# Layer 2 of a four-layer network: two fp32r parts of the projection weights instead of three bf16 parts, and one fp32r pass for dt

## The chip, the cores and the metric

The kernel runs on one core of a Trainium2 chip. The time is that of the device, in microseconds (us), from the first to the last instruction; less is better. Engines are TensorE (PE, matmuls; PEld is its weight load), VectorE (DVE), ScalarE (ACT), GpSimd (POOL) and SyncE (SP, which here only issues DMAs). ACT issues the DMAs of the set-up as well.

## The reference

Four layers follow one another on an input of 4 batches, 128 channels and 64 x 64 pixels. Layer 0 is attention over the 4096 pixels, layer 1 two quantized 3 x 3 convolutions, layer 2 a selective scan over the pixels as a sequence ("mamba"), layer 3 attention again. The change lies in layer 2:

```
xz = x @ W_in                                  # 128 -> 2 * 256
xh, z = split(xz, 2)
xh = silu(xp[:-1] * w[:, 0] + xp[1:] * w[:, 1] + b)   # causal convolution, two taps; xp is xh, padded
x_dbl = xh @ W_x                               # 256 -> 8 + 16 + 16
dt_low, Bmat, Cmat = x_dbl[:8], x_dbl[8:24], x_dbl[24:40]
dt = softplus(dt_low @ W_dt + b_dt)            # 8 -> 256
A = -exp(A_log)
h = exp(dt * A) * h + dt * Bmat * xh           # step by step, 16 states for each of 256 channels
y = (sum over the states of h * Cmat + xh * D) * silu(z)
x = silu(group_norm(y @ W_out)) + x_hsi
```

The input x of layer 2 is what layer 1 left: integers from 0 to 15 (divided by 15), which the kernel keeps exactly in fp8.

## The kernel before

Set-up (lines 161 to 335): constants are loaded on the DMA queue of ACT, in the order of the program, and prepared on DVE. `load_layer2` (L296) multiplies the first half of W_in by each of the two taps of the convolution, so that the projection and the convolution are one product over two shifted inputs, and splits the result `wf` (two tap products and the z half, 768 columns) into three bf16 parts `w3` (L309 to L312). `wf` and `cwb` take the two buffers of the tag "ud" in the pool `mam`. `w_dt` is cleared by POOL and gets W_dt twice, once for each half of a token block (L325 to L328).

The main part has no loops on the device. Generators describe chains of operations: `energies`, `exponentials`, `products`, `accumulations`, `parts` and `finish` for both attention layers; `convolutions` for layer 1; `preparation`, `decays`, `scans`, `lasts`, `additions` and `output` for layer 2; `images`, `fetches` and `stage_input` for DMAs. Each operation is announced by `op(engine, time, *needs)` with a time in us that the programmer put down. The class `Order` (L48) keeps a clock for each engine. Again and again it takes the operation with the earliest possible start, plus 0.15 times the rank of its chain, and emits it (L80 to L112). So the order on every engine is written at build time from these entries, and each engine then executes its list strictly in that order. The entry is no more than a planner's figure; if it changes, the order of everything changes. `bank=True` marks users of the one PSUM bank `ps_g`, of which only one is in work at a time; `port=True` keeps an operation of DVE off the operations of POOL.

Attention runs in stages of 64 blocks: (0, 0), (0, 1), (0, 2), (3, 0), (0, 3), (3, 1), (3, 2), (3, 3), given as (layer, batch). A block is eight energy products (L492), two exponentials on ACT (L511, 128 x 1024 each), eight products with v (L560) and, unless DVE adds the terms up (L533, only in the first eight column blocks and in the last stage), sums by matmul (L580). Four blocks make a column block of 256 queries, two column blocks an eviction (L606, L608) with sums turned into reciprocals: L627 on PE, L636 on DVE (`rall`), L640 on PE, L648 on DVE, and for layer 3 the output product L659 and L663. Stage (3, 3) needs x2 of batch 3, the output of layer 2 for the last batch.

Layer 2 goes through 32 token blocks of 512 (8 for each batch), each with 16 scan steps, one for each state. A scan step on DVE is the product with B (L1007), the product with C of the step before (L997) and two scans of 512 (L1015), with two decays on ACT ahead of them (L980) and an addition on POOL behind (L1032). `preparation` (L773) makes what a token block needs:

- z of the token block before: three bf16 products for each half of the channels (L764), copied by ACT (L787);
- xh of this one: six bf16 products for each half, with bias by ACT (L806), then Silu for both (L811, L814);
- x_dbl: eight instructions (L821); ACT copies it to `xd` (L830), SP writes B and C to DRAM (L835), from where `fetches` spreads them over the partitions (L967);
- dt: for each channel half two products of 256 tokens with `w_dt` (L851), in fp32, where one product appears as two instructions in the trace; softplus by ACT (L859 to L868) and DVE (L870 to L878).

`output` multiplies by W_out (`yo`, L894); after eight token blocks of a batch comes the group norm with Silu (L943), and x2 is written to DRAM (L958), from where `stage_input` reads it as `x_in` (L376).

## Time and profile before

| | us |
|---|---|
| median of 3 runs (3644.84 to 3651.89) | 3644.98 |
| span of the profiled execution | 3652.0 |
| PE busy, share of the span | 3375.5, 92% |
| DVE busy | 3124.9, 86% |
| ACT busy | 2505.9, 69% |
| POOL busy | 1317.5, 36% |
| scans of layer 2 on DVE (L1015), both forms | 1250.4 |
| energies and products of attention on PE (L492, L560, L580) | 2730.9 |
| products of the input projection (L764) | 148.3 |
| products for dt (L851) | 70.6 |

The profile shows one execution, whose span is the time meant in the prediction's sum. A group's line gives the line of the kernel, the engine, the operation, what it writes and reads, the shapes (for a matmul rows*columns of the weights first, then output columns and type), the count, then busy time in us and the mean of one in ns; behind the second bar stands how long the engine was idle just before such instructions, and what ended that. Matmuls overlap, so that count times mean is more than their busy time. A line of a timeline gives start and duration in us, engine, line, operation and count, in brackets the idle time ahead of it. A line of the waits gives total, times and longest. PEclk is the granted clock of PE as a share of full speed.

### The profile page before, as it was taken

To read this page: it belongs to the slowest core of one execution; us is meant where nothing else is said; L and a number is where in the kernel's file an instruction comes from. 1 tells how busy PE (TensorE), PEld (TensorE's weight loads), DVE (VectorE), ACT (ScalarE), POOL (GpSimd) and SP (SyncE) were. 2 spreads that over 40 slices of the span, in tenths; PEclk is the share of its full clock that TensorE was granted. 3 is DMA by queue.
4 is the path that set the end of the run, shared out by engine and by line. 5 is a ranking of instruction groups with operands and counts; after the bars stand their busy time and mean duration, and the time that the engine had idled before them with its cause. 6 is when DMAs were issued, how large, how long until landed. Compare 5 with 4: busy or idle time off the path is not lost.

```text
span 3652.0 us, 70191 instructions
## 1 busy us (share of the span) xinstructions
PE 3375.5 (92%) x29559; PEld 2217.0 (61%) x29559; DVE 3124.9 (86%) x2944; ACT 2505.9 (69%) x3655; POOL 1317.5 (36%) x567
## 2 busy tenths in 40 slices
PE   5999989999999899999988999999989999999998
PEld 3776656666666666655555666665555555565665
DVE  3369999999999999999999999999989999982333
ACT  3467777777677777777776777767777777864443
POOL 0014334444434444444444444443434444440000
PEclk8999999999999999999999999999999999999999
DMA  2013344343434434544433333333445544331000
GB/s 71 1 48 94 91 109 98 88 97 93 105 91 117 92 91 98 116 106 108 109 111 120 95 92 90 87 98 91 108 115 114 128 104 111 103 95 58 13 19 17
DMA packets 203655, 327.78 MB, mean 90 GB/s; under 512 B 50609, under 2 KB 53441, under 8 KB 203329
## 3 DMA queue, kind: packets, MB, share of 16 engines
q1 hardware_dynamic: 196384, 322.09, 35.4%
q8 instruction: 234, 3.83, 0.4%
q10 hardware_dynamic: 6944, 1.10, 0.2%
q14 instruction: 93, 0.75, 0.1%
HBM read 304.27 MB, written 18.87 MB: 88 GB/s over the span
## 4 chain that ended last, share of the span: by engine, by line
PE 50%; DVE 32%; ACT 9%; issue 6%; DMA 2%; ACTq 0%; DVEq 0%; SPq 0%
PE us L560 21%; DVE hs L1015 13%; PE e L492 12%; DVE hs L1007 7%; PE us L580 6%; DVE hs L997 5%; ACT da L980 2%; ACT p L511 2%; PE proj L463 2%; PE conv L675 1%; PE xh L764 1%; PE proj L421 1%; PE sc L627 1%; PE yo L894 1%; PE sc L640 1%
## 5 line engine op out<-in xcount | busy, mean ns | idle before, releaser
L1032 POOL TENSOR_TENSOR y<-y,hs 128x1024 f32<-128x1024 f32 x512 | 1219.6, 2382 | 1960.6 <-DVE hs L997 1941.9
L560 PE MATMUL us<-p,v 128*32 128x256 f32 (+1 forms) x12288 | 1519.1, 389 | 103.0 <-ACT p L511 74.1
L560 PEld LDWEIGHTS us<-p,v 128*32 128x32 f32 (+1 forms) x12288 | 1001.7, 138 | 519.2 <-issue 134.5
L511 ACT ACTIVATE p<-e 128x1024 f32<-128x1024 f32 x1024 | 1003.6, 1018 | 330.1 <-PE e L492 259.9
L1015 DVE TENSOR_TENSOR_SCAN hs<-da,hlast,hs 128x512 f32<-128x512 f32 x896 | 1100.8, 1264 | 15.7 <-ACT da L980 15.5
L980 ACT ACTIVATE da<-dt,amat 128x512 f32<-128x512 f32 x1024 | 703.1, 691 | 349.7 <-DVE hs L1015 346.0
L997 DVE TENSOR_TENSOR hs<-hs,bc 128x1024 f32<-128x1024 f32 x512 | 663.4, 1296 | 15.7 <-ACT hlast L990 15.5
L1007 DVE TENSOR_TENSOR hs<-ud,bc 128x1024 f32<-128x1024 f32 x512 | 661.4, 1292 | 0.2
L492 PE MATMUL e<-it,v 64*128 64x256 f32 x4096 | 529.2, 398 | 12.0 <-ACT p L511 11.1
L492 PEld LDWEIGHTS e<-it,v 64*128 64x128 f32 x4096 | 382.2, 191 | 160.8 <-issue 93.9
L580 PE MATMUL us<-p,ones 128*32 128x256 f32 x7040 | 471.0, 385 | 0.0
L580 PEld LDWEIGHTS us<-p,ones 128*32 128x32 f32 x7040 | 201.3, 110 | 189.0 <-issue 73.6
L492 PE MATMUL e<-it,j 64*128 64x256 f32 x2048 | 196.8, 309 | 12.0 <-ACT p L511 10.3
L492 PEld LDWEIGHTS e<-it,j 64*128 64x128 f32 x2048 | 140.9, 189 | 107.9 <-issue 71.6
L533 DVE TENSOR_TENSOR acc<-p 128x1024 f32<-128x1024 f32 x24 | 29.4, 1225 | 200.7 <-PE us L580 176.0
L533 DVE TENSOR_TENSOR acc<-p,acc 128x1024 f32<-128x1024 f32 x96 | 117.6, 1225 | 73.2 <-ACT p L511 68.2
L990 ACT COPY hlast<-hs 128x2 f32<-128x2 f32 x448 | 85.6, 191 | 122.7 <-DVE hs L1015 120.0
L1015 DVE TENSOR_TENSOR_SCAN hs<-da,hs 128x512 f32<-128x512 f32 x128 | 149.6, 1204 | 2.8 <-ACT da L980 2.7
L764 PEld LDWEIGHTS <-w 128*128 128x128 bf16 x576 | 52.5, 99 | 104.2 <-issue 61.9
L764 PE MATMUL xh<-x,w 128*128 128x512 fp8e4 x384 | 94.9, 383 | 7.9 <-ACT sz L787 4.2
L463 PE MATMUL proj<-L_conv_wvT,x_in 128*128 128x128 f32 (+1 forms) x512 | 71.3, 298 | 27.5 <-DVE it L408 17.8
L1036 POOL TENSOR_TENSOR y<-y,sz 128x1024 f32<-128x1024 f32 x32 | 94.4, 2951 | 2.5
(158 smaller groups left out, 2577.2 us busy)
## 6 DMA issues: line engine op xcount, KB each, us to landing
bc<-bc_d SPq DMA_DIRECT2D x512, 512.0 KB, 5.0
x_in<-in_x SPq DMA_DIRECT2D x16, 512.0 KB, 5.1
xpad<-in_x SPq DMA_DIRECT2D x32, 256.0 KB, 3.3
x_d<-yo SPq DMA_DIRECT2D x32, 256.0 KB, 3.0
x_in<-x_d SPq DMA_DIRECT2D x16, 512.0 KB, 6.3
o<-x_d SPq DMA_DIRECT2D x32, 256.0 KB, 5.2
out<-o SPq DMA_DIRECT2D x32, 256.0 KB, 2.0
bc_d<-xd SPq DMA_DIRECT2D x64, 32.0 KB, 1.8
```

The source lines that it names most:

```text
L463: nc.tensor.matmul(to[:, k * d : (k + 1) * d], lhsT=x[:, k // 4, k % 4 * P : (k % 4 + 1) * P], rhs=wv, start=True, stop=True,)
L492: nc.tensor.matmul(e[k % 4 // 2][:, k % 2, k // 4, :], lhsT=jts[s][row : row + D3, col : col + P], rhs=its[s][row : row + D3, c * CB : (c ...
L511: nc.scalar.activation(p, es[t][h], AF.Exp)
L533: nc.vector.tensor_add(accs[k], ps[t, h], other)
L560: nc.tensor.matmul(us[rows, 0, :], lhsT=vts[s][:, 8 * q + k, cols], rhs=ps[t, h][:, k % 2, k // 4, :], start=q == 0 and k < (1 if layer == ...
L580: nc.tensor.matmul(us[32 * m : 32 * m + 32, 1, :], lhsT=ones[:, 0:32], rhs=term, start=False, stop=q == NQ - 1 and k >= len(terms) - 4,)
L764: nc.tensor.matmul(g, lhsT=w3[:, k // len(rhs), lhs[k % len(rhs)] : lhs[k % len(rhs)] + P], rhs=x[:, rhs[k % len(rhs)]], start=(k == 0), s ...
L980: nc.scalar.activation(da, live["in", g][0][:, h, :], AF.Exp, scale=amat[:, h, n : n + 1])
L997: nc.vector.tensor_mul(hs, hs, bcs.pop(m)[:, 1:2, :].to_broadcast([P, 2, TB]))
L1007: nc.vector.tensor_mul(hs, ud, bcs[m][:, 0:1, :].to_broadcast([P, 2, TB]))
L1015: nc.vector.tensor_tensor_scan(hs[:, h, :], das.pop((m, h)), hs[:, h, :], hlast[:, n, h : h + 1] if g % NTB else 0.0, ALU.mult, ALU.add,)
L1032: nc.gpsimd.tensor_tensor(y, y, hss.pop(m), ALU.add)
```

## The change

The weights `wf` are split into two parts in fp32r, the high one rounded to this format and the low one the rest. The input goes to fp32r as well: ACT copies the 512 tokens of z and the 513 of xh from fp8 into `xf`, which takes the buffer "sp". z then needs two products for each half, xh four.

For dt, W_x has the eight columns of dt_low four times, so that x_dbl holds four equal groups of eight rows for each half of the block. ACT writes `xh` (the fp32r-rounded value in the groups where `lowx` is 1, zero elsewhere), DVE subtracts it from `xd` into `xp` in fp32r: high parts in two groups, low parts in the two others. `w_dt` has the high part of W_dt for two groups and the low part for the two others, so that one fp32r product adds all four combinations. The set-up gets the loads and operations that make this `w_dt`; its temporaries `wd` and `wh` take the buffers "ud" of `wf` and `cwb`. The clearing of `w_x` goes, since all its columns are now loaded. The running sum of attention, `acc`, shares the buffer "h". The planner's entries for z, xh and dt on PE become 0.5, 0.95 and 0.3 us.

```diff
--- before.py
+++ after.py
@@ -7,8 +7,6 @@
 from concourse._compat import with_exitstack
 
 F32 = mybir.dt.float32
-BF16 = mybir.dt.bfloat16
-
 FP8 = mybir.dt.float8e4
 
 
@@ -31,6 +29,7 @@
 DI = 256
 DS = 16
 DTR = 8
+RBC = 4 * DTR
 EPS = 1e-5
 LEVELS = 15.0
 
@@ -248,9 +247,8 @@
         nc.vector.tensor_mul(r, r, t)
 
     bn, wint = [], []
-    w3 = const.tile([P, 3, 3 * DI], BF16, tag="w3", name="w3")
+    w2 = const.tile([P, 2, 3 * DI], F32R, tag="w2", name="w2")
     w_x = const.tile([P, 2, D3], F32, tag="w_x", name="w_x")
-    nc.gpsimd.memset(w_x, 0.0)
     w_out = const.tile([P, 2, P], F32, tag="w_out", name="w_out")
     amat = const.tile([P, 2, DS], F32, tag="amat", name="amat")
 
@@ -306,14 +304,12 @@
         nc.vector.tensor_mul(wf[:, 0, :], wf[:, 1, :], cwb[:, 0, :])
         nc.vector.tensor_mul(wf[:, 1, :], wf[:, 1, :], cwb[:, 1, :])
         f = wf.rearrange("p a b -> p (a b)")
-        for k in range(3):
-            nc.vector.tensor_copy(w3[:, k, :], f)
-            if k < 2:
-                nc.vector.tensor_sub(f, f, w3[:, k, :])
-        nc.scalar.dma_start(
-            out=w_x[:, :, 0 : DTR + 2 * DS],
-            in_=i["L2_conv_W_x"].rearrange("(h p) r -> p h r", p=P),
-        )
+        nc.vector.tensor_copy(w2[:, 0, :], f)
+        nc.vector.tensor_sub(w2[:, 1, :], f, w2[:, 0, :])
+        wx = i["L2_conv_W_x"].rearrange("(h p) r -> p h r", p=P)
+        for k in range(4):
+            nc.scalar.dma_start(out=w_x[:, :, DTR * k : DTR * (k + 1)], in_=wx[:, :, 0:DTR])
+        nc.scalar.dma_start(out=w_x[:, :, RBC:D3], in_=wx[:, :, DTR : DTR + 2 * DS])
         nc.scalar.dma_start(out=w_out, in_=i["L2_conv_W_out"].rearrange("(h p) c -> p h c", p=P))
         nc.scalar.dma_start(out=amat, in_=i["L2_conv_A_log"].rearrange("(h p) n -> p h n", p=P))
         nc.scalar.activation(amat, amat, AF.Exp)
@@ -322,10 +318,27 @@
     load_layer1()
     load_layer2()
 
-    w_dt = const.tile([P, 2, DI], F32, tag="w_dt", name="w_dt")
-    nc.gpsimd.memset(w_dt, 0.0)
+    lowx = const.tile([P, 1], F32, tag="lowx", name="lowx")
+    nc.vector.tensor_reduce(
+        lowx, ident.rearrange("p (a k b) -> p k a b", k=2, b=DTR)[:, 1], AX.XY, ALU.add
+    )
+    w_dt = const.tile([P, 2, DI], F32R, tag="w_dt", name="w_dt")
+    wd = mam.tile([P, 2, DI], F32, tag="ud", name="wd", bufs=2)
+    wh = mam.tile([P, 2, DI], F32R, tag="ud", name="wh", bufs=2)
+    mhi, mlo = (const.tile([P, 1], F32, tag=k, name=k) for k in ("mhi", "mlo"))
+    nc.vector.tensor_reduce(
+        mlo, ident.rearrange("p (a k b) -> p k a b", k=2, b=2 * DTR)[:, 1], AX.XY, ALU.add
+    )
+    nc.vector.tensor_scalar(mhi, mlo, -1.0, 1.0, ALU.mult, ALU.add)
+    nc.gpsimd.memset(wd, 0.0)
     for k in range(2):
-        nc.scalar.dma_start(out=w_dt[k * D3 : k * D3 + DTR, k, :], in_=i["L2_conv_W_dt"])
+        for j in range(4):
+            r = k * D3 + j * DTR
+            nc.scalar.dma_start(out=wd[r : r + DTR, k, :], in_=i["L2_conv_W_dt"])
+    nc.vector.tensor_copy(wh, wd)
+    nc.vector.tensor_sub(wd, wd, wh)
+    nc.vector.tensor_scalar_mul(wh, wh, mhi)
+    nc.vector.scalar_tensor_tensor(w_dt, wd, mlo, wh, ALU.mult, ALU.add)
     cb, bdt, dpar = halves("L2_conv_conv_b"), halves("L2_conv_b_dt"), halves("L2_conv_D")
     gng, gnb = column("L2_conv_gn_gamma"), column("L2_conv_gn_beta")
     wq3r, wk3r = repeated("L3_conv_wqT", D3, D3, 1), repeated("L3_conv_wkT", D3, D3, 2)
@@ -528,7 +541,7 @@
                     need.append(("sums", t - 1))
                 yield op("DVE", 1.25, *need, port=True)
                 if q == 0:
-                    accs[k] = att.tile([P, 2, 2, CB], F32, tag="acc", name="acc", bufs=1)
+                    accs[k] = att.tile([P, 2, 2, CB], F32, tag="h", name="acc", bufs=1)
                 other = ps[t, 0] if q == 0 else accs[k]
                 nc.vector.tensor_add(accs[k], ps[t, h], other)
             mark("acc", t)
@@ -757,32 +770,31 @@
     def pair(name, tag, bufs):
         return mam.tile([P, 2, TB], F32, tag=tag, name=name, bufs=bufs)
 
-    def product(lhs, x, rhs, name):
+    def product(lhs, rhs, name):
         g = gtile(name)
-        n = 3 * len(rhs)
+        n = 2 * len(rhs)
         for k in range(n):
+            o = lhs[k // 2]
             nc.tensor.matmul(
-                g,
-                lhsT=w3[:, k // len(rhs), lhs[k % len(rhs)] : lhs[k % len(rhs)] + P],
-                rhs=x[:, rhs[k % len(rhs)]],
-                start=(k == 0),
-                stop=(k == n - 1),
+                g, lhsT=w2[:, k % 2, o : o + P], rhs=rhs[k // 2], start=(k == 0), stop=(k == n - 1)
             )
         return g
 
     def preparation():
         for g in range(NG + 1):
 
+            xf = None
             if g:
                 b, c = divmod(g - 1, NTB)
                 need = [("gated", g - 2)] if g > 1 else []
+                yield op("ACT", 0.69)
+                xf = mam.tile([P, 2 * TB + 1], F32R, tag="sp", name="xf")
+                nc.scalar.copy(xf[:, 0:TB], x1s[b % 2][:, 1 + c * TB : 1 + (c + 1) * TB])
                 for h in range(2):
-                    yield op("PE", 0.8, *need, ("begun", g - 1), bank=True)
+                    yield op("PE", 0.5, *need, ("begun", g - 1), bank=True)
                     if h == 0:
                         live["sz", g - 1] = sz = pair("sz", "sz", 1)
-                    ps = product(
-                        [2 * DI + h * P], x1s[b % 2], [slice(1 + c * TB, 1 + (c + 1) * TB)], "z"
-                    )
+                    ps = product([2 * DI + h * P], [xf[:, 0:TB]], "z")
                     yield op("ACT", 0.69)
                     nc.scalar.activation(sz[:, h, :], ps, AF.Copy, scale=1.0 / LEVELS)
                     release()
@@ -792,15 +804,16 @@
                 mark("sz", g - 1)
                 return
             b, c = divmod(g, NTB)
-            for h in range(2):
-                yield op("PE", 1.5, ("x1", b, c), bank=True)
+            yield op("ACT", 0.69, ("x1", b, c))
+            if xf is None:
+                xf = mam.tile([P, 2 * TB + 1], F32R, tag="sp", name="xf")
+            nc.scalar.copy(xf[:, TB:], x1s[b % 2][:, c * TB : 1 + (c + 1) * TB])
+            for h in range(2):
+                yield op("PE", 0.95, bank=True)
                 if h == 0:
                     xc = pair("xc", "xc", 1)
                 ps = product(
-                    [h * P, DI + h * P],
-                    x1s[b % 2],
-                    [slice(k + c * TB, k + (c + 1) * TB) for k in range(2)],
-                    "xh",
+                    [h * P, DI + h * P], [xf[:, TB + k : 2 * TB + k] for k in range(2)], "xh"
                 )
                 yield op("ACT", 0.69)
                 nc.scalar.activation(
@@ -828,13 +841,19 @@
             yield op("ACT", 0.43)
             xd = mam.tile([P, TB // 2], F32, tag="xd", name="xd")
             nc.scalar.copy(xd, ps[:, 0 : TB // 2])
+            yield op("ACT", 0.43)
+            xh = mam.tile([P, TB // 2], F32R, tag="xh", name="xh")
+            nc.scalar.activation(xh, ps[:, 0 : TB // 2], AF.Copy, scale=lowx)
             release()
+            yield op("DVE", 0.4, port=True)
+            xp = mam.tile([P, TB // 2], F32R, tag="xp", name="xp")
+            nc.vector.tensor_sub(xp, xd, xh)
             yield op("SP", 0.2, lag=0.1)
             bc_d = dram.tile([2, DS, TB], F32, tag="bc_d", name="bc_d")
             for k in range(2):
                 nc.sync.dma_start(
                     out=bc_d.rearrange("k n t -> (k n) t")[:, k * (TB // 2) : (k + 1) * (TB // 2)],
-                    in_=xd[k * D3 + DTR : k * D3 + DTR + 2 * DS, :],
+                    in_=xd[k * D3 + RBC : (k + 1) * D3, :],
                 )
             live["bc", g] = bc_d
             mark("bc_d", g)
@@ -842,7 +861,7 @@
 
             need = [("done", g - 2)] if g > 1 else []
             for h in range(2):
-                yield op("PE", 0.98, *need, bank=True)
+                yield op("PE", 0.3, *need, bank=True)
                 if h == 0:
                     dt, ud, y = (pair(t, t, 2) for t in ("dt", "ud", "y"))
                     a = pair("sp", "sp", 1)
@@ -851,7 +870,7 @@
                     nc.tensor.matmul(
                         ps[:, k * (TB // 2) : (k + 1) * (TB // 2)],
                         lhsT=w_dt[:, k, h * P : (h + 1) * P],
-                        rhs=xd,
+                        rhs=xp,
                         start=True,
                         stop=True,
                     )
```

## The prediction

> **What bounds the kernel now.** I read first the page's slices (VectorE, DVE, is near 99% from slice 3 to 35, TensorE, PE, near full all along), then the stretches that this suggests: up to the first scan step at 241 us, from there to the end of the last one at 3276.6, on to the first matmul of the last attention stage at 3331.4, and to the end.
>
> ```profile
> core 0: us, PE busy (x) PEld busy (x) DVE busy (x) ACT busy (x) POOL busy (x), PEclk, DMA share, GB/s
> 0.00:241.00 241.00, 193.19 (x1166) 146.26 (x1166) 89.64 (x142) 102.79 (x120) 3.54 (x23) 0.96 0.14 36
> 241.00:3276.60 3035.60, 2824.28 (x24109) 1845.28 (x24109) 2912.49 (x2663) 2231.65 (x3334) 1309.27 (x542) 0.97 0.41 102
> 3276.60:3331.40 54.80, 48.06 (x572) 29.44 (x571) 10.61 (x29) 28.80 (x36) 4.72 (x2) 0.94 0.19 70
> 3331.40:3652.00 320.60, 309.97 (x3718) 196.03 (x3716) 112.20 (x111) 142.65 (x168) 0.00 (x0) 0.99 0.06 19
> ```
>
> In the middle stretch DVE is busy 95.9%, PE 93.0%, ACT 73.5%. So the two first pace each other, and DVE has only 123 us to win. The head and tail belong to PE. Next, the waits of DVE in the middle stretch:
>
> ```profile
> DVE rall L636 <- PE sc L627: 45.1, 39, 3.2
> DVE hs L1015 <- ACT da L980: 18.3, 15, 3.0
> DVE hs L997 <- ACT hlast L990: 15.5, 22, 1.6
> DVE o L663 <- PE o L659: 10.4, 9, 3.7
> ```
>
> Only 58 us (45.1, 10.4 and 2.1 for L648) end on PE directly. Then the groups that the edit touches, and those that price it, shapes apart:
>
> ```profile
> L764 PE MATMUL xh<-x,w 128*128 128x512 fp8e4 x384 | 94.9, 383 | 7.9 <-ACT sz L787 4.2 <-ACT xc L806 3.2
> L764 PE MATMUL z<-x,w 128*128 128x512 fp8e4 x192 | 53.4, 388 | 16.6 <-ACT sz L787 15.3 <-ACT q L724 1.0 <-DVE us L648 0.2
> L851 PE MATMUL dt_ps<-xd,w_dt 128*128 128x256 f32 x256 | 70.6, 399 | 11.5 <-ACT dt L861 10.8 <-ACT yo L899 0.7
> L675 PE MATMUL conv<-xl,wint 128*128 128x512 f32 x224 | 58.8, 402 | 1.0 <-DVE xl L699 1.0
> L699 DVE TENSOR_TENSOR xl<-xpad,xh 128x660 fp32r<-128x660 f32 x32 | 30.7, 960 | 4.3 <-ACT xh L697 4.3
> ```
>
> Matmuls overlap, so busy divided by count prices one, not the mean. Last, the timelines of start and end:
>
> ```profile
> 36.15 1.17 ACTq L335 DMA_DIRECT2D wo<-in_L_conv_woT  x2
> 37.36 1.20 ACT L406 ACTIVATE h<-proj,lowb_i,low_i 128x1024 fp32r<-128x1024 f32 x1 [4.62 <-DMA L_conv_wvT<-in_L_conv_wvT]
> 43.20 1.28 DVE L408 SCALAR_TENSOR_TENSOR it<-proj,bq0r,h 128x1024 fp32r<-128x1024 f32 x1
> ```
>
> ```profile
> 3279.24 2.35 POOL L1036 TENSOR_TENSOR y<-y,sz 128x1024 f32<-128x1024 f32 x1
> 3286.89 1.98 PE L894 MATMUL yo<-y,w_out 128*128 128x512 f32 x4
> 3302.34 5.94 SPq L958 DMA_DIRECT2D x_d<-yo  x8
> 3311.31 3.74 PE L492 MATMUL e<-it,v 64*128 64x256 f32 x16
> 3331.48 1.88 PE L421 MATMUL proj<-x_in,L_conv_wkTr 128*128 128x512 f32 x4
> ```
>
> At the start ACT's first compute stands behind its own DMA issues. At the end, layer 3 of batch 3 starts 29 us after its input began to be written, since PE still works off batch 2.
>
> **What the Trainium skill says.** "TensorE: Matmul & The Clock Gate", weight-path perf modes: fast weight load is for non-FP32 weights. The trace agrees: bf16 loads of L764 take 99 ns, f32 and fp32r ones 189 to 192. The same page, part 1: after about 3.4 us of idleness the array runs at half rate for about as long; here the L492 group after 6 us of waiting took 3.74 us for the usual 2.00. "SBUF — State Buffer" (port contention): a VectorE operation with two SBUF inputs is blocked for the whole of a GpSimd operation reading SBUF. Here L699 takes 0.84 in the median and 2.86 at most, the difference nearly a POOL addition (2.38).
>
> **The change, part by part**, against the profiled 3652.0.
>
> *PE, saved.* 576 bf16 matmuls (148.3 us) become 384 fp32r ones. fp32r at the same shape costs 58.8/224 = 0.262 (xl) to 64.5/224 = 0.288 (xh of L675): 101 to 111, saving 37 to 48, I take 42. L851: 256 instructions, two passes each of 128, become 128. No row shows a full-height fp32r product of 256 columns; from below 196.8/2048 = 0.096 (L492 of layer 0, two halves side by side), from above 0.276 as now. I take the weight load, 0.19: 24 us, saving 46 (35 to 58). Together 88 us. This shortens the end only where PE sets the pace.
>
> *DVE, added: 32 xp subtractions of 256 columns.* Line through L699 (660 columns, 0.84) and L878 (1024 columns, 1.225): 1.06 ns a column and 0.14 fixed, so 0.41. POOL's lock adds what it adds to L699, mean minus median 0.12. 13 to 17 us, I take 15. Nothing hides it in a stretch where DVE is 96% busy.
>
> *The wait it brings.* xp waits for ACT's xh; behind it in DVE's queue stand scans and products, and on them ACT's decays and POOL. The same shape, L699 behind L697, waited 4.3 us in 32; L636 behind PE waited 76.9 in 64, or 1.2 each. Between 4 and 38; I take 5, since ACT releases it.
>
> *ACT, added.* 64 copies of 512 columns from SBUF at 0.69 to 0.72 (L980, L882) and 32 scaled reads at 0.47 (L606 with a gain): 60 us. It hides in ACT's waits, 335 us of them for DVE's scans at L980. Without that cover it reaches DVE through da and hlast (33.8 us of waits now): 0 to 10, I take 3.
>
> *Relief of DVE.* A shorter PE could take off at most the 58 us above. But the order refills the room: in the built instruction order of the changed kernel, attention's reciprocals stand about 11 scan steps earlier towards the end, so PE is filled rather than idle. 0 to 58, I take 15.
>
> *Moved from tail into middle.* In that order all 448 energy blocks of earlier stages precede the last yo; before, 443 did. So two more evictions come in DVE's middle: 2 x (0.18 + 0.68 + 0.68) = 3 us. Middle: 15 + 5 + 3 + 3 - 15 = +11 us.
>
> *Tail.* The five blocks that stood between the last scan and stage (3,3) are gone. yo starts at once after L1036 (3281.6, not 3286.9: 5 us). ACT no longer runs two exponentials and a table load between the square root and Silu (3296.2 to 3299.5, and one load more: 5 us). x2 would be out about 10 us earlier, at 3292; its landing (3) and the read back (6.3) bring the first projection to 3302 instead of 3331.5. Against this 29 I set 3 for a cold PE. -26 (from -20 to -32).
>
> *Head.* wd takes wf's buffer, so its clearing on POOL waits for DVE's last read of wf (the subtraction ending near 40.2). wd's eight loads stand in ACT's queue behind that, with amat's Exp and nine further DMAs (32.52 to 37.32: 4.8 us), and only then L406. 40.2 + 0.6 + 8 x 0.44 + 0.2 + 4.8 = 49.3, and `it` on DVE at 50.6, not 43.2: +7.4. It passes straight into a PE-bound head. At least +1 (four new operations less two casts and a subtraction on DVE), at most +12. The four further loads of w_x lie before the clearing is ready and cost nothing; alone they would be 1.8. In the first token block the copies and xh add 1.5 us of latency and PE's shorter steps take as much off.
>
> Other edits (w2's fp32 parts, the sum in h's buffer, the rows of bc_d) cost nothing: h is next written a stage later, and the DMA keeps its 32 rows of 1 KB.
>
> Sum: +7.4 + 11 - 26 = -7.6 us, that is 3644.4 against 3652.0, 0.21% less. The runs shown have their median at 3644.98, 7 below the profiled one: 3637.
>
> **The rivals.**
> *PE sets the middle's pace.* For it: PE ends the commonest DVE wait, and over half of the chain lies on PE. Against: DVE's share is the higher one. Net saving in the middle 88 less the five blocks brought forward (23) = 65. If half gets through: -33 - 26 + 7 = -52, 3593.
> *PE falls behind its written order, and DVE pays: slower.* The planner's new entries are 0.95, 0.5 and 0.3 us a step. With L675's rate and about 0.17 to fill (L764 now: six in 1.46), I get 1.2, 0.65 and 0.5, which is 1.1 us a token block, 35 in all, not contained in the order. Now its entries fit (0.8 and 1.5 against 0.81 and 1.46). If every bit arrives at L636 and xp, no relief remains: 7 + 15 + 5 + 3 + 3 + 35 - 26 = +42, 3687. It decides as soon as these waits grow by some 15 us. For it: L636 already waits 39 times of 51. Against: PE itself waits some 200 us in the middle (65 of them at L560 for exponentials), which can absorb it.
> *It doesn't deliver.* PE's lead is lost before the end, stage (3,2) still trails, and the tail gains only 8: 7 + 11 - 8 = +10, 3655.
>
> **How the numbers follow.** No change means within 0.2%, 7.3 us, which is about what a measurement of this kernel can tell. Forecast 0.42 (own range 3622 to 3652: 0.21 faster, 0.17 within, 0.04 just above); PE's pace 0.20, all faster; PE behind 0.28, slower; not delivered 0.10, slower. Faster 0.41, same 0.17, slower 0.42. Range 3593 to 3684: it leaves out about the lower half of the first rival and the upper part of the second.
>
> **What would show it.** Right: h at about 49 us; matmuls of L764's successor near 0.27 each; DVE's middle stretch about 11 us longer at some 96.5% busy; stage (3,3) beginning within 30 us of the last scan, after an idle PE. Wrong: a middle stretch over 25 us longer with more wait at L636's successor or at xp (second rival), or over 20 us shorter (first); blocks of batch 2 still on PE after the last yo (third).

## The result, and the profile after

The changed kernel takes 3669.43 us (median of 4 runs, 3668.5 to 3671.04), the kernel before 3647.9 (4 runs, 3644.84 to 3651.89): a ratio of 1.006, with a 95% interval from 1.0046 to 1.0074. It is slower by 21.5 us, where a gain of 8 was forecast. The spans of the two profiled executions, 3652.0 and 3666.6, differ by 14.6 only, since the one of before lies 4.1 above the median time of its runs and the one of after 2.8 below. The sums below are of spans of single executions, so that a difference of a few us between two of them says little; verdicts rest on the ratios.

First the stretches, as in the prediction: to the first scan step, to the end of the last scan, to the first projection of stage (3,3), and to the end (length, then busy time of PE, PEld, DVE, ACT, POOL, each with its count, then clock, DMA share, GB/s).

```profile
0.00:244.64 244.64, 190.94 (x1158) 145.49 (x1158) 91.44 (x148) 103.54 (x122) 3.57 (x22) 0.94 0.14 35
244.64:3320.59 3075.95, 2825.06 (x24361) 1868.12 (x24361) 2927.82 (x2699) 2294.87 (x3450) 1308.87 (x542) 0.97 0.38 101
3320.59:3344.83 24.24, 4.33 (x8) 1.97 (x9) 10.06 (x25) 9.11 (x12) 4.80 (x3) 0.57 0.24 79
3344.83:3666.60 321.77, 311.66 (x3713) 196.55 (x3713) 110.83 (x109) 143.96 (x169) 0.00 (x0) 0.98 0.07 22
```

Before, with the same borders (the middle ends at the last scan, 1.2 us earlier than in the prediction's table), the four are 241.0, 3034.4, 56.1 and 320.5 us. This is its middle:

```profile
241.00:3275.40 3034.40, 2823.08 (x24099) 1844.45 (x24101) 2911.30 (x2662) 2231.44 (x3333) 1309.15 (x542) 0.97 0.41 102
```

So the head is 3.6 longer, the middle 41.6 longer, the end 31.9 shorter and the last stage 1.3 longer. Nearly all hangs on the middle: DVE's busy time there grew by 16.5 (2911.3 before) and its idle time by 25 (length less busy: 123.1 before, 148.1 after).

Where it idles shows in the waits of DVE in the middle (total, times, longest):

```profile
DVE rall L649 <- PE sc L640: 40.5, 29, 7.8
...
DVE stats L926 <- ACT yo L918: 14.5, 1, 14.5
...
DVE o L676 <- PE o L672: 11.2, 9, 2.8
DVE xp L850 <- ACT xh L846: 5.8, 8, 1.6
```

The waits for PE (`rall`, `o`, `us`) are no longer in sum than before, 55.5 us against 57.6. New is one wait of 14.5 us. The starts of the first products with B of each token block (every sixteenth of L1007, now L1026) tell that up to token block 25 nothing is lost: it begins at 2649.0 us, 2647.6 before. Then token block 25 takes 130.4 us, not 102.2, and the six blocks behind it take 541.1, not 525.7. This is the end of token block 25, from the timeline of the three engines:

```profile
2732.93 0.12 DVE L241 TENSOR_SCALAR rs_v<-gv 128x1 f32<-128x1 f32 x1
...
2737.94 1.28 ACT L962 ACT_TABLE_LOAD   x1
2739.23 5.75 ACT L962 ACTIVATE yo<-yo,gsh,grs 128x512 f32<-128x512 f32 x8
2740.08 5.63 DVE L966 SCALAR_TENSOR_TENSOR yo<-x,yo 128x512 f32<-128x512 fp8e4 x8 [5.25 <-ACT yo L962]
...
2757.57 1.98 PE L913 MATMUL yo<-y,w_out 128*128 128x512 f32 x4
...
2760.20 0.69 DVE L926 BATCH_NORM_STATS2 stats<-yo 128x6 f32<-128x512 f32 x1 [14.50 <-ACT yo L918]
...
2778.13 1.22 DVE L897 TENSOR_TENSOR ud<-dt,xc 128x1024 f32<-128x1024 f32 x1
2779.45 1.23 DVE L1026 TENSOR_TENSOR hs<-ud,bc 128x1024 f32<-128x1024 f32 x1
```

The reader is to see a chain in which DVE has little to do for 46 us (it is busy 14 of them), from its last scan of block 25 (ended at 2733) to the first product of block 26. The group norm of batch 2 (square root, then Silu L962, then the additions L966 that make x2) stands in the instruction lists only behind the last scan step of block 25, that is at step 416 of 512. The product `yo` of token block 24 needs x2 of batch 2 (both are written in `output`), dt of block 26 needs that `yo`, and the first step of block 26, which is step 416, needs dt. Before, x2 stood at steps 405 to 407, with nine steps of scans behind it to cover the chain. ACT changes its table for each link, 1.28 us each time, as the Trainium skill states ("ScalarE activation tables: per-element evaluation and per-set limits", section "What a function is on this engine": 1283 ns between functions of different sets). The planner charges 1.3 us for such a change (LOAD in `Order`), so an operation with another table stands back while ACT has an exponential of attention ready.

PE is not idle meanwhile. Token block 25 before and after, in the columns of the stretches above:

```profile
2647.60:2749.80 102.20, 92.81 (x1038) 54.70 (x1036) 92.76 (x94) 77.43 (x117) 41.58 (x18) 0.93 0.45 115
2649.00:2779.40 130.40, 121.29 (x1426) 72.16 (x1424) 96.35 (x97) 93.95 (x137) 41.46 (x18) 0.96 0.35 97
```

PE has 28.5 us more of work in it, DVE 3.6. Blocks of attention stand in PE's list between the links of the chain: the last addition of x2 ended at 2745.7, but PE came to `yo` only at 2757.6, straight from attention. The late link and the attention that was brought forward thus stand in the same place.

Of the end, stage (3,3) begins after an idle PE, as was forecast:

```profile
3326.80 3.39 PE L913 MATMUL yo<-y,w_out 128*128 128x512 f32 x4 [10.50 <-POOL y L1055]
...
3344.83 3.78 PE L434 MATMUL proj<-x_in,L_conv_wkTr 128*128 128x512 f32 x4 [10.96 <-DMA x_in<-x_d]
```

### The profile page after: what moved, and what is told of

It reads as the page before. It is cut to its first block, busy times and chain, and to the rows that moved or that the text cites. A ratio compares the mean times of both kernels' runs of the same rounds, so it can differ in the third digit from the quotient of the medians.

```text
span 3666.6 us, 69715 instructions
## 1 busy us (share of the span) xinstructions
PE 3332.0 (91%) x29239; PEld 2212.1 (60%) x29239; DVE 3140.2 (86%) x2980; ACT 2551.5 (70%) x3751; POOL 1317.2 (36%) x566
## 4 chain that ended last, share of the span: by engine, by line
PE 48%; DVE 32%; ACT 9%; issue 7%; DMA 2%; POOL 0%; ACTq 0%; SPq 0%; DVEq 0%; POOLq 0%
PE us L573 21%; DVE hs L1034 13%; PE e L505 12%; DVE hs L1026 7%; PE us L593 6%; DVE hs L1016 5%; ACT da L999 2%; ACT p L524 2%; PE conv L688 1%; PE sc L653 1%; PE proj L434 1%; PE xh L778 1%; PE proj L476 1%; DVE q L743 1%; PE sc L640 1%
## 5 line engine op out<-in xcount | busy, mean ns | idle before, releaser
L1016 DVE TENSOR_TENSOR hs<-hs,bc 128x1024 f32<-128x1024 f32 x512 | 652.1, 1274 | 17.2 <-ACT hlast L1009 16.7
L1026 DVE TENSOR_TENSOR hs<-ud,bc 128x1024 f32<-128x1024 f32 x512 | 654.6, 1279 | 0.2
L505 PE MATMUL e<-it,v 64*128 64x256 f32 x4096 | 539.7, 403 | 14.3 <-ACT p L524 11.6
L476 PEld LDWEIGHTS proj<-L_conv_wvT,x_in 128*128 128x128 f32 x512 | 64.8, 206 | 44.7 <-issue 24.6
L640 PEld LDWEIGHTS sc<-sel,ss 128*128 128x128 f32 x512 | 66.3, 192 | 41.9 <-issue 18.6
```

What stands on the lines that cost most here:

```text
L476: nc.tensor.matmul(to[:, k * d : (k + 1) * d], lhsT=x[:, k // 4, k % 4 * P : (k % 4 + 1) * P], rhs=wv, start=True, stop=True,)
L505: nc.tensor.matmul(e[k % 4 // 2][:, k % 2, k // 4, :], lhsT=jts[s][row : row + D3, col : col + P], rhs=its[s][row : row + D3, c * CB : (c ...
L640: nc.tensor.matmul(sc[:, k : k + 1], lhsT=ss[:, k * P : (k + 1) * P], rhs=sel4, start=True, stop=True,)
L1016: nc.vector.tensor_mul(hs, hs, bcs.pop(m)[:, 1:2, :].to_broadcast([P, 2, TB]))
L1026: nc.vector.tensor_mul(hs, ud, bcs[m][:, 0:1, :].to_broadcast([P, 2, TB]))
```

## The experiments

Thirteen kernels were run, each beside the kernel before on the same chip; four chips were used, on which the kernel before had medians of 3647.9 to 3651.4 us, so that ratios compare better than times. In the table, "middle" is the time from the first product of a scan step to the end of the last scan, "end" from there to the first projection of stage (3,3), "idle" the middle less DVE's busy time in it. The letter a stands for the whole change, b for the kernel before, p for the projection part alone, d for the dt part alone.

| kernel | ratio to before, 95% interval | middle | end | idle |
|---|---|---|---|---|
| before | 1 | 3034.4 | 56.1 | 123.1 |
| after | 1.0060, 1.0046 to 1.0074 | 3076.0 | 24.2 | 148.1 |
| a_sqrt | 1.0027, 1.0020 to 1.0034 | 3065.9 | 32.5 | 138.0 |
| a_rank0 | 1.0085, 1.0071 to 1.0099 | 3092.1 | 24.5 | 171.8 |
| b_late | 1.0041, 1.0027 to 1.0055 | 3072.6 | 32.2 | 157.9 |
| b_sqrt | 1.0001, 0.9993 to 1.0010 | 3033.8 | 56.2 | 128.4 |
| a_frozen | 1.0063, 1.0049 to 1.0076 | 3045.7 | 56.1 | 117.0 |
| p_frozen | 0.9992, 0.9983 to 1.0000 | 3024.7 | 56.2 | 114.1 |
| d_frozen | 1.0074, 1.0061 to 1.0088 | 3051.8 | 56.2 | 122.4 |
| d_nosub | 1.0018, 1.0011 to 1.0024 | 3036.0 | 56.0 | 123.6 |
| p_only | 1.0072, 1.0059 to 1.0086 | 3085.7 | 24.4 | 170.2 |
| p_late24 | 1.0008, 1.0002 to 1.0015 | 3068.7 | 23.1 | 156.4 |
| p_lateS12 | 1.0059, 1.0046 to 1.0072 | 3090.8 | 24.9 | 180.6 |
| p_early22 | 0.9972, 0.9962 to 0.9982 | 3046.3 | 32.4 | 140.4 |
| p_early16 | 1.0024, 1.0015 to 1.0033 | 3062.7 | 32.6 | 156.0 |

**The late group norm: taken away, and put into the kernel before.** The first theory was that the late group norm is the loss. In the changed kernel and in the kernel before, the table charge of its square root was taken away:

```diff
-            yield op("ACT", 0.5, table="sqrt")
+            yield op("ACT", 0.5)
```

> The changed kernel with one planner's argument taken away: the square root of the group norm is no longer charged 1.3 us for its ACT table, so that the end of batch 2's group norm is written at scan step 391.5 and not 416. Theory (the late group norm starves DVE between token blocks 25 and 26): token block 25 falls from 130 us to about 102, and the whole from about 3669 to 3641 us (3634 to 3648), a ratio of 0.996 to 1.000 to the kernel before. Rival (the loss is the dearer PE steps and the new DVE and ACT work, spread over all token blocks): 3664 to 3674 us, ratio 1.005 to 1.007.

> The kernel before with the table charge of the square root taken away, as a control: its group norm of batch 2 moves from step 405 to 389, where it starves nobody in either order. Both theories: within 7 us of the kernel before (3641 to 3655 us). A larger difference would mean that any rearrangement of the order moves the time by as much as the loss to be explained.

In the kernel before, the square root of batch 2 was made to wait:

```diff
-            yield op("ACT", 0.5, table="sqrt")
+            yield op("ACT", 0.5, *([("s", 415, 1)] if b == 2 else []), table="sqrt")
```

> The kernel before with one need added: the square root of batch 2's group norm must wait for scan step 415, so that it is written at step 416, as in the changed kernel; nothing of the change itself is in it. Theory: token block 25 takes about 125 to 130 us instead of 102 and the whole is 20 to 30 us longer, 3668 to 3678 us (ratio 1.005 to 1.008). Rival: the late group norm is harmless, 3643 to 3653 us (ratio within 0.002 of 1).

And in the changed kernel, the output chain got another rank:

```diff
-        (3, output()),
+        (0, output()),
```

> The changed kernel with the output chain of layer 2 at rank 0 instead of 3, another way to an early group norm (batch 2 ends at scan step 388.5). Theory: about the same as with the table charge taken away, 3632 to 3650 us. Rival (spread loss): 3662 to 3676 us.

With the late square root alone, the kernel before loses 34.4 us in token block 25 (136.6, 102.2 before) and no more than 2 us in any other; the idle times on DVE in that block are of the kind shown above (its timeline):

```profile
2748.35 0.18 DVE L636 RECIPROCAL rall<-sc 128x4 f32<-128x4 f32 x1 [8.33 <-PE sc L627]
...
2764.09 0.69 DVE L907 BATCH_NORM_STATS2 stats<-yo 128x6 f32<-128x512 f32 x1 [7.44 <-ACT yo L899]
...
2781.75 1.23 DVE L870 SCALAR_TENSOR_TENSOR y<-y,sp 128x1024 f32<-128x1024 f32 x1 [16.96 <-ACT ud L868]
```

So a late group norm does make such a hole. But it does not come alone: in this order, too, all blocks of the earlier attention stages stand ahead of the last `yo`, and the energy products in token block 25 (L492) grow from 242 instructions to 386. The end became 24 us shorter by it (56.1 to 32.2), since PE works off blocks of attention while DVE idles, and the time grew by 0.41%, less than expected. (Of the 17.8 us that the span of its profiled execution is longer than that of before, 3.3 lie in the head, where its list is that of before.) The control did not move (1.0001). In the changed kernel the early group norm took token block 25 back to 92.7 us, yet the other blocks together became 27.6 longer, and only about half of the loss went (1.0060 to 1.0027; 3661.2 us, where 3641 was expected): the middle stayed 31 us above that of before, and of the end's gain 8 were lost. With rank 0 the loss grew (3683.9, where 3632 to 3650 was expected): x2 of batch 2 stands at 390 there, but DVE waits 14.1 and 17.0 us for softplus (L889 <- ACT ud L887), another link of layer 2 written late. The late group norm explains where most of the middle's growth stands, not why the kernel is slower.

**The same work in the old order.** The planner kept the old entries and the new operations went in unplanned: an operation with time None is emitted as soon as its needs are written, and touches no clock of the planner. The lists of old operations are then those of before, operation for operation, except in the set-up.

```diff
+            for item in self.chains:
+                while item[3] and item[3][1] is None and all(k in self.marks for k in item[3][2]):
+                    item[3] = next(item[1], None)
...
-                yield op("ACT", 0.69)
+                yield op("ACT", None, *need, ("begun", g - 1))
...
-                    yield op("PE", 0.5, *need, ("begun", g - 1), bank=True)
+                    yield op("PE", 0.8, *need, ("begun", g - 1), bank=True)
...
-                yield op("PE", 0.95, bank=True)
+                yield op("PE", 1.5, ("x1", b, c), bank=True)
...
-            yield op("DVE", 0.4, port=True)
-            xp = mam.tile([P, TB // 2], F32R, tag="xp", name="xp")
-            nc.vector.tensor_sub(xp, xd, xh)
...
+            yield op("DVE", None)
+            xp = mam.tile([P, TB // 2], F32R, tag="xp", name="xp")
+            nc.vector.tensor_sub(xp, xd, xh)
...
-                yield op("PE", 0.3, *need, bank=True)
+                yield op("PE", 0.98, *need, bank=True)
```

> The whole change, but in the order of the kernel before: the planner keeps its old entries and the new operations (copies to xf, xh, xp) are put in their chains without being planned, so that every engine runs the old list with the new work in between. First theory (the rearranged order makes the loss; the change's own work costs DVE its 21 us of subtractions, some 5 us of waiting and 3 us of set-up, and gives back about 30 us at the end): last scan at about 3305, span 3646 to 3656, ratio 0.998 to 1.002. Rival (the change's own work is what costs, whatever the order): ratio 1.004 to 1.007 as in the changed kernel.

> The projection part alone (fp32r weights in two parts, copies to xf; dt stays in fp32) in the order of the kernel before. First theory: PE loses 70 us of work, DVE gets none; the last scan stays at 3275 to 3280, stage (3,3) starts some 23 us behind it and not 55, span 3620 to 3630, ratio 0.991 to 0.995. Rival (the 44 us of copies on ACT reach DVE): last scan 3290 or later, ratio 0.997 or more.

> The dt part alone (four row groups, xh and xp, one fp32r pass) in the order of the kernel before. First theory: DVE carries 21 us of subtractions and about 5 us of waits, set-up 3 us later: last scan at about 3304, PE's 35 us less cover that at the end, span 3646 to 3656, ratio 0.998 to 1.002. If the subtraction's wait costs more than its own time, 1.003 or more; if PE's relief pays for it, 0.996 or less.

> The projection part alone with the planner's new entries for z and xh, so in an order of its own (batch 2's group norm ends at scan step 397). If the order that the planner writes is what decides, it stands anywhere from 3625 to 3660 and clearly above the same part in the old order; if only the work counts, within 5 us of that.

The middle and the end of the whole change in the old order, then of its projection part alone in the old order:

```profile
244.62:3290.36 3045.74, 2774.08 (x23787) 1835.67 (x23789) 2928.74 (x2693) 2270.97 (x3427) 1312.48 (x542) 0.97 0.38 102
3290.36:3346.45 56.09, 49.34 (x585) 30.37 (x582) 11.79 (x29) 29.01 (x36) 4.86 (x3) 0.94 0.19 69
```

```profile
239.69:3264.36 3024.67, 2797.53 (x23911) 1857.24 (x23913) 2910.57 (x2662) 2260.28 (x3396) 1313.04 (x542) 0.98 0.38 102
3264.36:3320.54 56.18, 49.43 (x585) 30.29 (x582) 11.79 (x30) 29.02 (x36) 4.87 (x3) 0.94 0.19 68
```

Two readings. First, the end is 56 us in every kernel with the old order, with PE 49 busy in it, however much work PE was spared: these blocks of attention are written behind the last scan, and no saving on PE moves them. I had expected the end to shrink by PE's relief, and it didn't; so p_frozen gained 0.08% and not the 0.5 to 0.9% that I expected, and d_frozen lost 0.74%, beyond its range too. Second, the whole change costs the same in the old order as in its own (1.0063 and 1.0060). That is what the rival to my first theory had said: the loss is the cost of the change's own work, and the new order gives about what it takes. It takes 31.9 us from the end and adds 30.2 to the middle (3045.7 to 3076.0). As good as all of these 30.2 are idle time of DVE (117.0 to 148.1): its busy time is the same in both orders (2928.7 and 2927.8), although the subtractions, which the planner doesn't keep off POOL's operations when they are unplanned, take 24.4 us in all in the old order and 21.8 in the new one. Token block 25 alone is as much longer (100.2 to 130.4), while the other blocks gain and lose. By its own planner the projection part is 28.5 us dearer than in the old order (3672.60 against 3644.09; 3625 to 3660 was expected): there x2 of batch 1 stands at step 288, the last at which it can, and token block 17 takes 133.2 us, not 107.1.

The parts add up: by medians against the runs beside them, the projection part is worth -3.8 us (3644.09 less 3647.91), the dt part costs 25.9 (3673.82 less 3647.91), both together 21.6.

**What in the dt part costs.** In the dt part alone, in the old order, the subtraction and with it the low parts of x_dbl are left out:

```diff
-            yield op("DVE", None)
-            xp = mam.tile([P, TB // 2], F32R, tag="xp", name="xp")
-            nc.vector.tensor_sub(xp, xd, xh)
...
-                        rhs=xp,
+                        rhs=xh,
```

> The dt part alone in the old order, without the subtraction on DVE: xp and the low parts of x_dbl are left out, and the fp32r product reads xh; set-up, copies on ACT and PE's 35 us less stay. Theory (DVE is at its floor in the middle, so that the subtractions pass into the time and PE's relief does not): of the 26 us that the dt part costs, some 20 go; 3649 to 3656 us, ratio 1.000 to 1.002. Rival (waits for ACT's new copy, or the four loads of W_x and the dearer set-up, are the cost): 3664 us or more, ratio 1.004 or more.

3657.74 against 3651.38: 6.4 us remain of 25.9, so 19.5 belong to the subtractions on DVE and their waits, by medians from two chips. The middle gives 15.8, without them first, with them second:

```profile
245.51:3281.51 3036.00, 2796.03 (x23975) 1822.22 (x23977) 2912.39 (x2662) 2240.70 (x3364) 1310.43 (x542) 0.97 0.42 102
```

```profile
245.24:3297.04 3051.80, 2801.41 (x23975) 1824.53 (x23977) 2929.44 (x2693) 2242.37 (x3364) 1312.13 (x542) 0.97 0.38 101
```

15.8 us of length go with 17.0 of DVE's work, and its idle time is as good as the same (123.6 and 122.4). Without the subtraction the middle is that of before (3036.0 and 3034.4), although PE has 27 us less work in it. The remaining 6.4 are the set-up for the larger part: its middle begins at 245.5, not 241.0.

**Both gains at once?** The blocks behind the last scan can come earlier if the planner thinks PE cheaper, and the projection part alone leaves DVE's work as it was. From token block 24, 22, 16 or 12 on, smaller entries (0.5 and 0.95 from blocks 24 and 12 on, 0.35 and 0.7 from 22 and 16 on) were put in the projection part in the old order, in all but the first of these kernels together with the uncharged square root:

```diff
-                    yield op("PE", 0.8, *need, ("begun", g - 1), bank=True)
+                    yield op("PE", 0.35 if g >= 22 else 0.8, *need, ("begun", g - 1), bank=True)
...
-                yield op("PE", 1.5, ("x1", b, c), bank=True)
+                yield op("PE", 0.7 if g >= 22 else 1.5, ("x1", b, c), bank=True)
...
-            yield op("ACT", 0.5, table="sqrt")
+            yield op("ACT", 0.5)
```

> The projection part alone in the old order up to token block 24; from there the planner has the smaller entries for z and xh (0.5 and 0.95), so that the blocks of attention which stood behind the last scan come before it; batch 2's group norm ends at scan step 405.5. Theory (end and middle can be had apart: the middle has room on PE, and only a late group norm costs DVE): stage (3,3) begins 24 to 32 us after the last scan instead of 56, the middle grows by under 10 us, 3615 to 3632 us, ratio 0.991 to 0.996. Rival (work moved from the end into the middle is paid back there in full, as in the changed kernel): 3640 to 3650 us, ratio 0.998 or more.

> The projection part alone, the smaller entries from token block 12 on, and no table charge for the square root (group norms end at scan steps 137, 262 and 393.5). Theory: stage (3,3) begins 24 to 30 us after the last scan; the group norms are early but the new order costs DVE up to 20 us spread over the blocks, as in the changed kernel with its charge taken away: 3625 to 3645 us, ratio 0.994 to 0.999. Rival as for the run before: 0.999 or more.

> The projection part alone in the old order up to token block 22, then smaller entries for z and xh (0.35 and 0.7), and no table charge for the square root. The additions of x2 of batch 2 stand at scan steps 390 to 392, and from token block 25 on every ud is written two to nine scan steps before it is needed. Theory (DVE runs dry only where such a link of layer 2 is written at its last permitted step: x2 at 416 in the changed kernel, in the one with the late square root and in the one with smaller entries from block 24, each 31 to 36 us more in token block 25): no token block from 24 on is more than 10 us longer than in the projection part alone, stage (3,3) starts 32 to 45 us after the last scan, not 56, and the time is 3622 to 3638 us (ratio 0.993 to 0.997). Rival (whatever is moved from the end into the middle is paid there in full): 3642 us or more, ratio 0.998 or more.

> As the run before, with the smaller entries from token block 16 on: x2 of batches 1 and 2 at scan steps 262 to 264 and 390 to 391, and every ud from block 16 on two to nine steps early. Theory: 3620 to 3640 us (ratio 0.993 to 0.998), no token block over 10 us longer but those that now hold a group norm. Rival: ratio 0.998 or more.

In p_late24 the square root was early enough, but the Silu behind it was not: x2 stands at step 416 again, and token block 25 takes 129.9 us (98.8 in p_frozen). I had looked at the square root alone. In p_lateS12 a wait of 17.5 us for softplus (L871 <- ACT ud L869) stands in block 28. p_early22 has no such link from token block 24 on and has the lowest ratio of all, 0.28% under the kernel before, just short of the 0.3 to 0.7% expected:

```profile
240.26:3286.60 3046.34, 2829.43 (x24229) 1875.22 (x24231) 2905.90 (x2665) 2271.91 (x3411) 1315.71 (x542) 0.97 0.40 102
3286.60:3319.04 32.44, 22.50 (x267) 13.56 (x265) 10.89 (x28) 16.00 (x22) 4.89 (x3) 0.89 0.21 67
```

Against p_frozen the end is 23.7 us shorter, and the middle 21.7 longer, of which 18.8 in block 24 and 8.9 less in block 25 (the group norm moved from the second into the first), and 0 to 5 more in each later block. The last stage is 2.1 longer (322.1 and 319.9), so that the two profiled spans are alike, 3641.1 and 3640.5; that p_early22 is faster than p_frozen rests on ratios from two chips alone (0.9972 and 0.9992). So without a late link most of what is moved was still paid in the middle; p_early16 paid 38. The other three came out in the range of their rivals. The theory that only late links cost is thereby wrong as it was put: the holes that hold them are the largest single piece, but against the same work in the old order every order tried here that shortened the end cost the middle at least 0.85 of what it took from the end (20.2 for 23.6 in a_sqrt; 21.7 for 23.7 in p_early22; 44 for 33 in p_late24). What this remainder hangs on, and whether some order avoids it, stays open. No run has a late link without attention brought forward beside it, so the share of each in a hole is open as well.

## Why the prediction failed

By its own steps, against the profiled execution:

| step | forecast | measured |
|---|---|---|
| head | +7.4 | +3.6 |
| xp's subtractions and their waits, ACT, relief (the work itself, middle) | +15 +5 +3 -15 = +8 | +11.3 (a_frozen) |
| the new order in the middle, with the blocks moved from the end | +3 | +30.2 (after less a_frozen) |
| end and last stage | -26 | -31.9 +1.3 |
| sum | -7.6 | +14.6 |

The step that failed is "Moved from tail into middle". I saw in the built order that five blocks come forward, priced them at the two evictions that they bring to DVE, 3 us, and booked the 26 us at the end as a gain. The end did pay (-31.9), but the order that brings the blocks forward cost the middle 30.2, nearly all of it idle time of DVE and not the evictions that I had priced. The step took for granted that DVE's written list has no hole while PE does 51 us more of attention beside it (2774.1 us of PE work in the middle of a_frozen, 2825.1 in that of after), and it did not ask where in the new order each batch's group norm stands; that x2 of batch 2 had moved from 405 to 416, the last possible place, could have been read in the same list. The experiments show that a token block with x2 at this place is 26 to 34 us longer wherever it occurs (after, b_late, p_late24, and p_only one batch earlier), and also that a better place doesn't make the move free.

Without the 3 and the 26, the prediction's own terms give +15.4 us; the change in the old order measured +13.7 by spans (3665.7 and 3652.0) and 21.6 by medians.

The mechanism for the work itself was right: DVE is the bound of the middle. That its sum in the middle came close (+8 and +11.3 by spans) is in part luck, since single terms were off both ways. The subtractions took 21.8 us in all and not 13 to 17. Shapes apart, the lines of the changed kernel that answer to those of the prediction:

```profile
L778 PE MATMUL xh<-xf,w 128*128 128x512 f32 x256 | 77.8, 425 | 6.6 <-ACT xf L810 4.1 <-ACT yo L918 1.6 <-ACT q L737 0.7
L778 PE MATMUL z<-xf,w 128*128 128x512 f32 x128 | 48.7, 462 | 12.7 <-ACT sz L799 12.0 <-DVE us L661 0.3 <-ACT q L737 0.3
...
L870 PE MATMUL dt_ps<-xp,w_dt 128*128 128x256 f32 x128 | 35.5, 360 | 21.4 <-DVE xp L850 11.5 <-ACT dt L880 8.3 <-DVE us L661 0.8
...
L850 DVE TENSOR_TENSOR xp<-xd,xh 128x256 fp32r<-128x256 f32 x32 | 21.8, 680 | 6.3 <-ACT xh L846 6.3
```

The subtraction's median is 0.426 us, close to the 0.41 of the line through two sizes, but its mean is 0.68 and its longest 2.44. The trace shows where the rest comes from:

```profile
1730.05 2.37 POOL L1051 TENSOR_TENSOR y<-y,hs 128x1024 f32<-128x1024 f32 x1 [2.96 <-DVE hs L1016]
1730.26 2.44 DVE L850 TENSOR_TENSOR xp<-xd,xh 128x256 fp32r<-128x256 f32 x1 [0.35 <-ACT xh L846]
```

Thirteen of the 32 subtractions take 0.50 us or more. Each of them begins while an operation of POOL runs, and ends 0.28 us after it; the other 19 take 0.40 to 0.43. This agrees with what the Trainium skill states ("SBUF — State Buffer", "Who interferes with whom") of a VectorE instruction with two SBUF inputs beside a GpSimd instruction that reads SBUF, and it costs twice what I took from L699 (mean less median 0.25, not 0.12). The waits at xp were 5.8 us here and 8.9 in a_frozen, where I took 5. The relief was nearly as forecast in the old order, where DVE's waits for PE (`rall`, `o`, `us`) in the middle fell from 57.6 to 46.2, 11 against 15; in the kernel's own order they hardly fell (55.5). From the waits of DVE in the middle of a_frozen:

```profile
DVE rall L654 <- PE sc L645: 39.8, 35, 2.7
...
DVE xp L864 <- ACT xh L851: 8.9, 8, 3.8
DVE o L681 <- PE o L677: 5.8, 8, 1.8
```

The 3 us for ACT don't show: there DVE's waits for decays and `hlast` fell from 33.8 to 29.1 us. (ACT's cover for its new work, its waits at L980 for the scans, was 346 us before, not the 335 of the prediction.) On PE I was too hopeful: 384 fp32r products took 126.5 us, saving 22, not 42, and dt's 128 took 35.5, saving 35, not 46; the 0.19 a product that I chose for dt was wrong, and the upper bound of 0.276 right (35.5/128 = 0.277). It changed little, as PE's time is not the bound.

In the head the direction was right, at half the size (the six kernels with the new set-up for dt begin their first scan at 244.4 to 245.5 us, the others at 238.5 to 241.4, but for the 244.3 of b_late). The wait is in the trace, but for an earlier operation:

```profile
36.66 0.62 POOL L333 MEMSET wd<- 128x512 f32 x1 [32.86 <-DVE wf L305]
...
45.25 1.21 ACT L419 ACTIVATE h<-proj,lowb_i,low_i 128x1024 fp32r<-128x1024 f32 x1 [6.48 <-DMA L_conv_wvT<-in_L_conv_wvT]
46.49 1.28 DVE L421 SCALAR_TENSOR_TENSOR it<-proj,bq0r,h 128x1024 fp32r<-128x1024 f32 x1 [1.81 <-ACT h L419]
```

POOL waited for the tap product (L305), the last reader of `cwb`, at 36.6, not for the subtraction near 40.2; so `wd` seems to lie in the buffer of `cwb` and not of `wf`. The first `h` came at 45.25 and not at 49, and `it` 3.3 us later than before (46.49 and 43.20), not 7.4.

Of the rivals, PE does not set the middle's pace: in p_frozen it has 25.5 us less work in the middle, and the middle is 9.7 shorter in the profiled execution, the whole kernel 3.8 by medians. The rival that ended slower named PE behind its written order, with longer waits at the reciprocals and at xp; the first did not grow (40.5, 45.1 before), the second was about what the forecast itself had (5.8). The result lies on its side for other reasons, the change's own work on DVE and in the head, and holes in the written order that take back the gain at the end. The third rival, that the end doesn't shorten, is refuted (56.1 to 24.2).

## What to carry to other kernels

Where a build-time planner writes the order, run a change twice: once with the old order held fixed, which prices its work, and once as planned; the difference is the order's. Here it was near nothing in sum, yet made of two parts of some 30 us, each larger than the change's own cost. Before booking work moved from one stretch into another as a gain, look for every chain with a latest place (here the group norm between two batches) and see how many steps of cover are left to it in the new list. And time taken off one engine by giving its neighbour more is worth nothing if the neighbour is the one at its floor: here 35 us less on PE were bought with 16 to 20 us on DVE, at full price.

## What was not expected of the hardware

An fp32r product of 128 x 512 took 0.30 (xh) and 0.38 us (z) of busy time on average, the bf16 one before 0.25 and 0.28 (94.9/384 and 53.4/192), so going from three products to two saved 15% of PE's time for the projection, not a third. A VectorE subtraction of 256 columns took anything from 0.40 to 2.44 us, by what was left of POOL's running operation when it began (0.28 us more than that, in all thirteen long ones). The small subtraction lost more by this than the larger one by which it had been priced: on average 0.25 us over the median, L699 0.12, of whose ten starts within an operation of POOL eight fell into its last 0.25 us. And a longer stall is not lost time for the other engines: of the 34 us that the late square root cost DVE, PE gave back 24 at the end.
